# A graph layer on one core: the iota behind the adding gathers of maxima is left out

## The chip, the cores and the metric

The kernel runs on one core of one Trainium2 chip. The metric is the device time of one execution in microseconds (us), from the start of the program to its end. The profile is that of one execution; its span runs from the first to the last instruction.

The core's engines work beside each other, each through its own list of instructions, in order: TensorE (PE; PEld is its weight load), VectorE (DVE), ScalarE (ACT), GpSimd (POOL) and SyncE (SP), which here only issues DMAs. Where one needs another's result it waits on a semaphore.

## The reference

There are 6250 nodes with 256 features and 100000 edges, sorted by destination. For each edge a row of messages is made, and each node takes the maximum over its incoming edges. Then follow a residual sum and a layer norm. Cut to what matters:

```python
x_src = x[src]
x_dst = x[dst]
theta_x = (x_dst - x_src) @ theta_w.T + theta_b
phi_x = x_src @ phi_w.T + phi_b
e = relu(theta_x + phi_x)
out = segment_max(e, dst, num_segments=6250)
out = where(isfinite(out), out, 0.0)
y = x + out
return (y - mean(y)) / sqrt(var(y) + 1e-5)
```

A message is `relu(x_dst @ theta_w.T + x_src @ (phi_w - theta_w).T + theta_b + phi_b)`. The first product is the same for all edges into a node. So the kernel computes B = x @ (phi_w - theta_w).T once for each node, takes the maximum of B's rows over the edges, and adds the other product and the biases to that maximum.

## The kernel before, in words

**Rows of B.** At the start x is loaded, transposed and multiplied, and B is stored to the DRAM tensor `b_rows`. B's rows for single edges are then fetched by gathers: `gather` (L542) issues one indirect DMA on GpSimd's queue, 128 rows of 256 float32 (1 KB each), one row into each partition, chosen by a column of indices.

**Two kinds of nodes.** The first 618 nodes ("part 1" in the code) have their edges cut into 128 chunks of 80 steps; each step is one gather (`gather_group`), and VectorE runs a maximum along the steps (L712). The results go to the DRAM tensor `maxima_1`. The other 5632 nodes are 44 tiles of 128. For these, most edges are handled without a gather: in "slots" of 383 rows of B, at most one edge of each node is picked for each slot, a one-hot matrix is made from the picked rows' codes (ScalarE L1243 and L1247, VectorE L1241), TensorE multiplies it (L1192), and VectorE takes the maximum into `acc` (L1206). What edges are left over form "the list": 128 chunks of 256 steps, again one gather (L543, g<-b_rows,list_src) and one maximum (L712) for each step, stored to `maxima_2`.

**Final part.** For each tile of 128 nodes, `rows_of` (L1465) fetches the node's maximum. Its target is first filled with the bias row (ScalarE, L1478); then a gather with `onto=ALU.add` adds the row of `maxima_1` or `maxima_2` that belongs to each node onto it. These are the *adding gathers*. There are 44 for the tiles of the second kind (g<-maxima,place in the profile), and 5 for the nodes of the first part (x_f<-maxima,place), which `first_shares` (L1707) interleaves with the list. All other gathers use `ALU.bypass`, which copies: the plain gathers.

Then `piece` handles two tiles at a time: TensorE multiplies the transposed x by theta (L1513) and turns `acc` back to rows (L1522), VectorE takes the larger of the gathered row and `acc` (L1523), adds the product (L1524), and adds the relu of it onto x with the row's sum (L1527). `normalise` (L1535) takes squares on ScalarE (L1556), the inverse root on VectorE with a square root on ScalarE (L437 to L444), scales (L1571 on ScalarE, L1567 on VectorE) and stores (L1577; the last share L1551). The shares of the final part are 8, 8, 8, 4, 4, 4, 4, 2 and 2 tiles; loads of x (L1483) and of the transposed x (`kept`, L1463) and the stores go through SyncE's queue.

**What sets the order on GpSimd.** `in_turn` ties each of GpSimd's instructions to the one before, so that they stand as they are written. Behind each gather, from the fifth group of the first part on (`paused[0]`, set in `gather_group`), `gather` puts an iota of 128x160 into a tile `pause` that nobody reads:

```python
pause = const.tile([P, PAUSE], FP, name="pause")
...
if paused[0]:
    in_turn(iota(pause, 1, 0, 0))
```

The profile shows it as IOTA pause (L511, the line of the helper `iota`). Since `paused[0]` stays set, the list's gathers and the adding gathers have it as well.

Of the kernel before, what the change touches and what calls it, by code (L numbers as in the profile page):

```python
# [46 lines left out]
ALU = mybir.AluOpType  # L47
# [400 lines left out]
def gnn_kernel(ctx: ExitStack, tc: tile.TileContext, x, src, dst, theta_w, theta_b, phi_w, phi_b, out):  # L448
# [61 lines left out]
    def iota(t, step, base, per_partition):  # L510
        return nc.gpsimd.iota(  # L511
            t,
            pattern=[[step, t.shape[1]]],
            base=base,
            channel_multiplier=per_partition,
            allow_small_or_imprecise_dtypes=True,
        )
# [9 lines left out]
    def in_turn(one):  # L527
        if latest[0] is not None:
            behind_in_order(one, latest[0], "GpSimd's order")
        latest[0] = one.ins.name  # L530
# [9 lines left out]
    paused = [False]  # L540

    def gather(to, table, offsets, wait_for=None, onto=ALU.bypass):  # L542
        one = nc.gpsimd.indirect_dma_start(  # L543
            out=to, out_offset=None, in_=table, in_offset=bass.IndirectOffsetOnAxis(ap=offsets, axis=0), compute_op=onto
        )
        in_turn(one)
        if wait_for is not None:
            after = mybir.DependencyInfo(mybir.DependencyClass.Sync, mybir.DependencyReason.DATA)
            tc.add_manual_dep(one.ins, wait_for, after, reason="rows that are used")
        issued = latest[0]  # L550
        if paused[0]:
            in_turn(iota(pause, 1, 0, 0))
        return issued

# [15 lines left out]
    def gather_group(i, table, a=0, b=STEPS):  # L570
        paused[0] = i >= PAUSED_FROM
        t0, n = groups[i]
        if i not in ring_tiles:
            ring_tiles[i] = gathered.tile([P, STEPS, D], FP, name="g")
        return [
            gather(ring_tiles[i][:, k, :], table, src_1[:, t0 + k : t0 + k + 1], hold(k)) for k in range(a, min(b, n))
        ]
# [856 lines left out]
    def gather_2(g, t0, a, b):  # L1434
        for k in range(a, b):
            t = LIST_CHUNK - 1 - t0 - k
            gather(g[:, k, :], b_rows, list_src[:, t : t + 1], hold(k))

    def gather_carry():

        carry_row = work.tile([P, D], FP, name="heads", bufs=1)
        gather(carry_row, maxima_2[: 1 + CARRY_GROUPS * STEPS * P, :], carry_at)
        return carry_row
# [408 lines left out]
```

## Time and profile before

| | |
|---|---|
| median of 3 runs | 765.55 us (761.78 to 767.07) |
| the profiled execution | 763.97 us |
| its span | 762.1 us |
| mean granted TensorE clock | 0.948 |
| GpSimd busy | 593.8 us, 78% of the span |
| adding gathers of the final part | 44, from 651.86 us to 741.09 us |

The page gives each engine's busy time, the span in 40 slices, the DMA queues, the chain of work that ended last (followed back from the last instruction, at each step to what released it), and the costliest groups of instructions. A group's row reads: line, engine, operation, what is written <- what is read, x count | busy us, mean ns of one | idle time of the engine ahead of them, and what ended most of it. A row of the timeline reads: start us, duration us, engine, line, operation, tiles, count, and in brackets the idle time ahead of it with its releaser; "issue" is time in which the engine waited for nothing that the profile shows. In rows of waits, "A <- B: 32.5, 15, 4.9" is A waiting for B, in total 32.5 us, 15 times, the longest 4.9 us.

A gather's duration in these rows is the time in which GpSimd issues it. The rows land later; that shows in who waits for them.

### The profile page before, as it was taken

To read this page: it belongs to the slowest core of one execution; us is meant where nothing else is said; L and a number is where in the kernel's file an instruction comes from. 1 tells how busy PE (TensorE), PEld (TensorE's weight loads), DVE (VectorE), ACT (ScalarE), POOL (GpSimd) and SP (SyncE) were. 2 spreads that over 40 slices of the span, in tenths; PEclk is the share of its full clock that TensorE was granted. 3 is DMA by queue.
4 is the path that set the end of the run, shared out by engine and by line. 5 is a ranking of instruction groups with operands and counts; after the bars stand their busy time and mean duration, and the time that the engine had idled before them with its cause. 6 is when DMAs were issued, how large, how long until landed. Compare 5 with 4: busy or idle time off the path is not lost.

```text
span 762.1 us, 9846 instructions
## 1 busy us (share of the span) xinstructions
PE 650.9 (85%) x2837; PEld 525.4 (69%) x2837; DVE 634.4 (83%) x1201; ACT 506.3 (66%) x687; POOL 593.8 (78%) x778
## 2 busy tenths in 40 slices
PE   5898796999989999999898797898887999976730
PEld 3787685878767888888776676676676877865520
DVE  5999899999999999998777787789777987754565
ACT  1444579788985879888766676668475866624545
POOL 7010489998958888888888889888888887799980
PEclk9999999999998999999999998999999999998965
DMA  8896544566469786777777888679678767478763
GB/s 252 286 343 253 177 126 143 150 195 207 152 197 296 238 304 210 244 249 238 244 226 227 269 249 255 198 223 299 210 244 292 243 219 231 92 151 238 168 143 144
DMA packets 66411, 168.22 MB, mean 221 GB/s; under 512 B 11910, under 2 KB 28206, under 8 KB 60206
## 3 DMA queue, kind: packets, MB, share of 16 engines
q1 hardware_dynamic: 40338, 107.92, 41.4%
q0 software_dynamic: 23744, 52.50, 26.5%
q10 hardware_dynamic: 2268, 7.11, 2.5%
q8 instruction: 24, 0.39, 0.2%
q14 instruction: 37, 0.30, 0.1%
HBM read 104.25 MB, written 63.23 MB: 220 GB/s over the span
## 4 chain that ended last, share of the span: by engine, by line
POOL 33%; DVE 22%; PE 18%; issue 12%; DMA 11%; ACT 2%; POOLq 0%; DVEq 0%; ACTq 0%
POOL g L543 25%; PE ps_f L1192 18%; DMA g<-b_rows,list_src 7%; POOL pause L511 7%; DVE g L712 4%; DVE acc L1206 4%; DVE words L1021 2%; DMA g<-maxima,place 2%; DVE hot L1241 2%; DVE work L1018 1%; ACT x_f L1571 1%; DVE work L1376 1%; POOL x_f L543 1%; DVE unused L1083 1%; DMA want<-chosen_rows 1%
## 5 line engine op out<-in xcount | busy, mean ns | idle before, releaser
L1192 PE MATMUL ps_f<-hot,terms 128*128 128x512 f32 x2112 | 507.2, 400 | 44.5 <-DVE acc L1206 32.5
L1192 PEld LDWEIGHTS ps_f<-hot,terms 128*128 128x128 f32 x2112 | 402.7, 193 | 142.6 <-DVE acc L1206 38.2
L543 POOL DMA_INDIRECT g<-b_rows,list_src x256 | 265.1, 1036 | 44.4 <-issue 36.8
L1243 ACT ACTIVATE hot<-want,minus_row 128x1024 fp32r<-128x1024 f16 (+1 forms) x201 | 208.2, 1070 | 110.4 <-PE ps_f L1192 92.6
L1206 DVE SCALAR_TENSOR_TENSOR acc<-ps_f,bias_column,acc 128x1024 f32<-128x1024 f32 (+1 forms) x192 | 227.8, 1190 | 6.4 <-PE ps_f L1192 4.2
L712 DVE SCALAR_TENSOR_TENSOR g<-g,caps 128x256 f32<-128x256 f32 x334 | 159.5, 480 | 59.1 <-DMA g<-b_rows,list_src 43.4
L1247 ACT ACTIVATE hot<-hot 128x1024 fp32r<-128x1024 f32 (+1 forms) x201 | 187.4, 973 | 1.1
L511 POOL IOTA pause<- 128x160 f32 x354 | 140.1, 396 | 2.1
L543 POOL DMA_INDIRECT g<-b_rows,src x72 | 110.2, 1531 | 27.7 <-issue 14.7
L543 POOL DMA_INDIRECT g<-maxima,place x44 | 69.3, 1576 | 13.7 <-issue 7.0
L1241 DVE TENSOR_SCALAR hot<-want,row_id 128x1024 fp32r<-128x1024 f16 (+1 forms) x93 | 67.9, 731 | 6.1 <-PE ps_f L1192 3.8
L811 PE MATMUL ps_b<-weights_b,x_t 128*128 128x256 f32 x228 | 53.8, 390 | 5.4 <-ACT x_t L799 5.2
L811 PEld LDWEIGHTS ps_b<-weights_b,x_t 128*128 128x128 f32 x228 | 43.1, 194 | 12.6 <-ACT x_t L799 7.1
L1513 PE MATMUL ps_f<-weights,kept 128*128 128x256 f32 x128 | 36.2, 432 | 14.3 <-DVE g L1524 8.1
L1513 PEld LDWEIGHTS ps_f<-weights,kept 128*128 128x128 f32 x128 | 26.2, 215 | 19.8 <-issue 15.9
L1556 ACT ACTIVATE squares<-x_f,r 128x256 bf16<-128x256 f32 x47 | 23.2, 494 | 21.2 <-DVE r L1553 21.2
L1523 DVE TENSOR_TENSOR g<-g,ps_f 128x512 f32<-128x512 f32 x16 | 11.0, 686 | 28.6 <-DMA g<-maxima,place 27.7
L1571 ACT ACTIVATE x_f<-x_f,r 128x256 f32<-128x256 f32 x40 | 21.0, 589 | 16.9 <-DVE r L1563 16.8
L814 ACT COPY b_sb<-ps_b 128x512 f32<-128x512 f32 (+1 forms) x25 | 14.4, 578 | 26.4 <-PE ps_b L811 17.8
L1023 POOL MEMSET work<- 128x1584 f32 x1 | 2.3, 2254 | 33.6 <-DVE words L1021 33.6
L799 ACT COPY x_t<-ps_xt 128x512 f32<-128x512 f32 (+1 forms) x29 | 16.1, 584 | 7.8 <-PE ps_xt L795 6.2
L1153 ACT CAST terms<-raw 128x768 fp32r<-128x768 f32 x16 | 13.2, 822 | 11.4 <-PE ps_f L1192 7.3
(275 smaller groups left out, 464.6 us busy)
## 6 DMA issues: line engine op xcount, KB each, us to landing
maxima<-g SPq DMA_DIRECT2D x41, 1024.0 KB
want<-chosen_rows SPq DMA_DIRECT2D x89, 256.0 KB
x_q<-in_x_dram SPq DMA_DIRECT2D x12, 512.0 KB
b_rows<-b_sb ACTq DMA_DIRECT2D x12, 512.0 KB
x_columns<-x_t SPq DMA_DIRECT2D x22, 256.0 KB
kept<-x_columns SPq DMA_DIRECT2D x11, 512.0 KB
raw<-b_rows SPq DMA_DIRECT2D x16, 256.0 KB
g<-b_rows,list_src POOLq DMA_INDIRECT x256
```

The source lines that it names most:

```text
L511: return nc.gpsimd.iota(t, pattern=[[step, t.shape[1]]], base=base, channel_multiplier=per_partition, allow_small_or_imprecise_dtypes=True,)
L543: one = nc.gpsimd.indirect_dma_start(out=to, out_offset=None, in_=table, in_offset=bass.IndirectOffsetOnAxis(ap=offsets, axis=0), compute_ ...
L712: one = nc.vector.scalar_tensor_tensor(g[:, k, :], last[part], caps[:, t : t + 1], g[:, k, :], op0=ALU.min, op1=ALU.max)
L811: nc.tensor.matmul(ps[:, h, :], x_t[:, h, k, :], weights_b[:, k, :], start=(k == 0), stop=(k == KC - 1))
L1192: one = nc.tensor.matmul(ps[:, w : w + 512], terms[:, part, b, h * P : (h + 1) * P], hot[b][:, w : w + 512], start=(i == 0), stop=(i == n ...
L1206: one = nc.vector.scalar_tensor_tensor(to, ps, bias_column[:, h : h + 1], to, op0=ALU.add, op1=ALU.max)
L1241: nc.vector.tensor_scalar(hot[b], want, row_id[:, b : b + 1], None, op0=ALU.is_equal)
L1243: one = nc.scalar.activation(hot[b], want, AF.Abs, bias=minus_row[:, b : b + 1], scale=1.0)
L1247: nc.scalar.activation(apart, apart.bitcast(FP), AF.Relu, bias=1.0, scale=-1.0)
L1513: nc.tensor.matmul(a[:, i, :], x_t[:, 2 * i + c, :], weights[:, c, :], start=(c == 0), stop=(c == KC - 1))
L1556: nc.scalar.activation(squares, x_f[:, k, :], AF.Square, bias=mean[:, k : k + 1], scale=1.0, accum_out=var[:, k : k + 1])
L1571: nc.scalar.activation(x_f[:, k, :], x_f[:, k, :], AF.Identity, bias=mean[:, k : k + 1], scale=inv[:, k : k + 1])
```

## The change

The iota is issued only behind gathers that copy. Behind the adding gathers it is left out; the gathers themselves, their targets and their order stay.

```diff
         issued = latest[0]
-        if paused[0]:
+        if paused[0] and onto == ALU.bypass:
             in_turn(iota(pause, 1, 0, 0))
         return issued
```

This takes 49 of the 354 iotas of `pause` away. GpSimd's order, where the list ends and the final part begins (`maxima_66` is `maxima_2`, `place_704` the places of the nodes' maxima in it); before:

```order
L543 DMA g<-b_rows,list_src 128x256
L511 IOTA pause 128x160
L543 DMA g<-maxima_66,place_704 128x256
L511 IOTA pause 128x160
L543 DMA g<-maxima_66,place_704 128x256
```

and with the change, to the end of the main program (the last two rows read the flag that decides on the general path):

```order
L543 DMA g<-b_rows,list_src 128x256
L511 IOTA pause 128x160
L543 DMA g<-maxima_66,place_704 128x256 x44
L1820 TENSOR_LOAD flags
L1821 COMPARE_AND_BRANCH
```

The 44 adding gathers, an iota between each two before, now follow each other.

In the list stage, on GpSimd too, four of the five adding gathers of the first part's nodes stand together (`maxima_65` is `maxima_1`); with the change:

```order
L543 DMA g<-b_rows,list_src 128x256
L511 IOTA pause 128x160
L543 DMA x_f<-maxima_65,place_703 128x256 x4
L543 DMA g<-b_rows,list_src 128x256
L511 IOTA pause 128x160
```

The iota in front of the four belongs to the list's gather before them; the next one stands behind the list's first gather after them.

## The prediction

> **What bounds the kernel now.** I read the page of the profile first, then GpSimd's own rows over the final part, then who waits for whom there, then the last microseconds. The page gives the span, and the chain of work that ended last.
>
> ```profile
> span 762.1 us, 9846 instructions
> POOL 33%; DVE 22%; PE 18%; issue 12%; DMA 11%; ACT 2%; POOLq 0%; DVEq 0%; ACTq 0%
> POOL g L543 25%; PE ps_f L1192 18%; DMA g<-b_rows,list_src 7%; POOL pause L511 7%; DVE g L712 4%; DVE acc L1206 4%; DVE words L1021 2%; DMA g<-maxima,place 2%; DVE hot L1241 2%; DVE work L1018 1%; ACT x_f L1571 1%; DVE work L1376 1%; POOL x_f L543 1%; DVE unused L1083 1%; DMA want<-chosen_rows 1%
> ```
>
> A third of the chain is GpSimd (POOL), and the iota itself ("pause") has 7% of it. The chain covers all stages, though, and the change touches only the adding gathers, so the stage has to be read by itself. GpSimd's groups from 651.8 to 741.5 us:
>
> ```profile
> L543 POOL DMA_INDIRECT g<-maxima,place x44 | 69.3, 1576 | 13.7 <-issue 7.0 <-ACT hot L1243 6.5 <-ACT x_f L1571 0.2
> L511 POOL IOTA pause<- 128x160 f32 x44 | 38.2, 869 | 0.0
> ```
>
> All 44 adding gathers of the final part lie here, one iota behind each; apart from the 6.5 us ahead of the first one, GpSimd is idle only for the "issue" gaps, 7.0 us over 42 gathers. So nothing holds GpSimd up once it has begun; it runs at its own pace. Who waits for that pace (waits from 651.8 to 745 us):
>
> ```profile
> DVE g L1523 <- DMA g<-maxima,place: 32.5, 15, 4.9
> PE ps_f L1513 <- DVE g L1524: 8.1, 4, 3.1
> ```
>
> VectorE (DVE) works off the rows in 22 pieces of two gathers, and in 15 of the 22 it stands still until the rows have landed, 32.5 us in all. TensorE in turn waits for VectorE to give back its PSUM buffers. Last, the end, in order of time:
>
> ```profile
> 739.53 1.56 POOL L543 DMA_INDIRECT g<-maxima,place  x1 [0.17 <-issue]
> 740.53 0.87 POOL L511 IOTA pause<- 128x160 f32 x1
> 744.46 0.69 DVE L1523 TENSOR_TENSOR g<-g,ps_f 128x512 f32<-128x512 f32 x1 [2.85 <-DMA g<-maxima,place]
> ```
>
> VectorE has been idle for 2.85 us when the last gather's rows are there; 762.1 - 744.5 = 17.6 us of normalising and storing follow. The final part is therefore: 44 gathers at GpSimd's pace, one landing, and a tail of fixed length.
>
> **The change, part by part.** It removes 49 iotas of 128x160, 44 in the final part and 5 behind the gathers into x_f in the list stage, and adds nothing. No wait is added.
>
> First the price of one iota. The recorded 869 ns is not it, as the order of time shows:
>
> ```profile
> 653.92 1.57 POOL L543 DMA_INDIRECT g<-maxima,place  x1 [0.17 <-issue]
> 654.92 0.87 POOL L511 IOTA pause<- 128x160 f32 x1
> 655.95 1.56 POOL L543 DMA_INDIRECT g<-maxima,place  x1 [0.17 <-issue]
> ```
>
> The first gather ends at 653.92 + 1.57 = 655.49; the iota begins on paper at 654.92, inside the gather, and ends at 655.79. Only 0.30 us of it lies behind the gather; then come 0.17 us until the next gather starts. Start to start is 2.03 us, of which 0.30 + 0.17 = 0.47 is not gather.
>
> The Trainium skill, page "Perfetto Trace Analysis", section "GPSIMD Engine Instruction", says to time GpSimd's instructions by the spacing of their starts and not by the recorded duration; the rows above agree (0.87 us recorded, 0.30 outside the gather). By the recorded mean the 43 iotas between gathers would be 37.4 us and the kernel would come to 728.2 us.
>
> What takes the place of the 0.47 us when gather follows gather directly? No adding gather does so in this trace. The nearest rows are plain gathers at the program's start, where no iota stands between:
>
> ```profile
> 5.54 0.95 POOL L543 DMA_INDIRECT g<-in_x_dram,src  x1 [0.30 <-issue]
> 6.79 0.95 POOL L543 DMA_INDIRECT g<-in_x_dram,src  x1 [0.30 <-issue]
> 8.05 0.95 POOL L543 DMA_INDIRECT g<-in_x_dram,src  x1 [0.30 <-issue]
> ...
> 636.88 0.96 POOL L543 DMA_INDIRECT g<-b_rows,list_src  x1 [0.16 <-issue]
> 637.85 0.28 POOL L511 IOTA pause<- 128x160 f32 x1
> 638.29 0.96 POOL L543 DMA_INDIRECT g<-b_rows,list_src  x1 [0.16 <-issue]
> ```
>
> Gather behind gather needs a gap of 0.30 us, start to start 1.25. With the iota it is 1.41. For a plain gather of the same length, the iota costs 1.41 - 1.25 = 0.16 us net, since taking it away brings back a longer issue gap. Applied to the adding gather: 0.47 - 0.30 = 0.165 us. Below, the price of one removed iota is bounded by nothing (the gap grows to 0.47); above by 0.47 (gathers close up altogether). I take 0.165, because the two rows differ from the case in the gather's length alone and the iota's part behind the gather is the same in both, 0.28 and 0.30.
>
> The final part: 43 of the 44 iotas lie between gathers (the one at 740.53 is behind the last and delays nobody): 43 x 0.165 = 7.1 us. The last gather would end at 741.09 - 7.1 = 734.0.
>
> Does what stands behind keep up? A piece would come every 2 x 1.86 = 3.7 us instead of 4.05. VectorE's work for a piece is two operations of 128x512 and two of 128x256, from these groups of the final part:
>
> ```profile
> L1523 DVE TENSOR_TENSOR g<-g,ps_f 128x512 f32<-128x512 f32 x15 | 10.3, 686 | 25.8 <-DMA g<-maxima,place 24.8 <-PE ps_f L1522 0.9
> L1524 DVE TENSOR_TENSOR g<-g,ps_f 128x512 f32<-128x512 f32 x15 | 10.3, 685 | 0.3
> L1527 DVE SCALAR_TENSOR_TENSOR x_f<-g,x_f 128x256 f32<-128x256 f32 x42 | 16.4, 421 | 0.4
> ```
>
> That is 0.69 + 0.69 + 2 x 0.42 = 2.2 us, so 1.5 us of slack are left per piece. Busy times of the two halves of the stage, and of the tail (the columns are PE, PEld, DVE, ACT and POOL busy, TensorE's clock, DMA share, GB/s):
>
> ```profile
> 652.00:700.00 48.00, 40.16 (x192) 33.38 (x190) 27.03 (x75) 21.12 (x48) 44.15 (x48) 0.93 0.70 147
> 700.00:741.00 41.00, 21.88 (x98) 17.25 (x96) 24.21 (x92) 17.42 (x55) 37.66 (x42) 0.83 0.75 178
> 741.00:762.10 21.10, 0.00 (x0) 0.00 (x0) 10.48 (x62) 11.33 (x34) 0.39 (x2) 0.50 0.44 146
> ```
>
> If the second stretch shrinks from 41.0 to 37.7, VectorE is busy 24.2 of it, ScalarE 17.4 and TensorE 21.9; none becomes the bound. TensorE is full early in the first stretch, because leftovers of the slots are multiplied there, but that backlog is gone by the middle. What hides an unfinished piece is VectorE's wait; it shrinks by about a fifth (7.1 of 32.5) and stays. I therefore let the whole 7.1 us reach the end.
>
> The five iotas in the list stage, of which one and four lie behind x_f gathers:
>
> ```profile
> 471.82 1.56 POOL L543 DMA_INDIRECT x_f<-maxima,place  x1 [0.17 <-issue]
> 472.82 0.87 POOL L511 IOTA pause<- 128x160 f32 x1
> 473.85 1.56 POOL L543 DMA_INDIRECT x_f<-maxima,place  x1 [0.17 <-issue]
> ```
>
> The spacing is the same 2.03 us, so 5 x 0.165 = 0.8 us of GpSimd's time. GpSimd is not always the bound there: the chain also runs through landings and VectorE's steps. Between 0 and 0.8 I take 0.4.
>
> Sum: 7.1 + 0.4 = 7.5 us. The span goes from 762.1 to 754.6; with the 1.9 us around it (763.97 - 762.1) the profiled execution would take 756.5. That execution is 1.6 us below the median of the runs shown, 765.55, so against the median I forecast 765.55 - 7.5 = **758.0 us**, a change of 0.98%.
>
> **The rivals.** *Absorbed by the transfers.* A gather's rows land 2.3 to 6.6 us after its end. The two ends of that:
>
> ```profile
> 698.64 1.56 POOL L543 DMA_INDIRECT g<-maxima,place  x1 [0.17 <-issue]
> 706.79 0.69 DVE L1523 TENSOR_TENSOR g<-g,ps_f 128x512 f32<-128x512 f32 x1 [2.93 <-DMA g<-maxima,place]
> ...
> 715.19 1.56 POOL L543 DMA_INDIRECT g<-maxima,place  x1 [0.17 <-issue]
> 719.09 0.69 DVE L1523 TENSOR_TENSOR g<-g,ps_f 128x512 f32<-128x512 f32 x1 [1.88 <-DMA g<-maxima,place]
> ```
>
> Issued until 716.75 and used at 719.09 the second; the first issued until 700.20 and used at 706.79, while tiles of x and of its transposed copy are being loaded. If denser gathers queue up behind such loads to the end, part of the gain goes. For it speaks the DMA share of 0.75; against it, that the lag is back at 744.46 - 741.09 = 3.4 by the last gather. With half the gain lost: 765.55 - 3.75 = 761.8 us.
>
> *The gathers overlap.* The iota starts 0.99 us after its gather's start, inside it. If the next gather may start as early, the 0.30 us gap is hidden too. With half of it hidden, the spacing is 1.71 and the gain 43 x 0.315 = 13.5 us: 752.0 us; fully hidden, 43 x 0.465 = 20 us: 745.6. Against it: behind the iota's early start the spacing repeats at 2.03 without anything running ahead, which looks as if a gather starts only when all before it is complete. The Trainium skill, same page and section, says there is no synchronisation between GpSimd's DSPs except inside instructions, which speaks for this rival.
>
> *Gathers without a gap get slower.* The first part has 25 gathers in a row without iotas (83.9 to 134.6 us), and then 40 with them (134.6 to 214.4 us):
>
> ```profile
> L543 POOL DMA_INDIRECT g<-b_rows,src x25 | 43.4, 1734 | 16.3 <-DMA b_rows<-b_sb 8.9 <-issue 7.3
> L543 POOL DMA_INDIRECT g<-b_rows,src x40 | 59.5, 1488 | 6.6 <-issue 6.6
> ```
>
> The unspaced ones take 0.25 us more. If an adding gather grows as much, its spacing is 1.58 + 0.25 + 0.30 = 2.13, 0.1 above today's: 43 x 0.1 = 4.3 us slower, 769.9 us. It turns the sign as soon as a gather grows by over 0.165 us. Against it: these stretches have different work beside them, and the gathers from x shown above, unspaced as well, take 0.95 us.
>
> That the change does not do what it says is excluded by the order of the instructions: the 44 gathers stand in one run without an iota, and VectorE, TensorE and SyncE keep their sequence.
>
> **How the numbers follow.** Forecast 0.66, with its own range of 6 to 9 us gained, which is 756.5 to 759.6; absorbed 0.15; overlap 0.12; slower 0.07. One per cent is 7.7 us, about what a measurement of this kernel can tell from no change, and the forecast sits right below it. Faster by over 1%: all of the overlap and under half of the forecast, 0.12 + 0.30 = 0.42. Slower by over 1% (a gather growing by 0.35 us) gets 0.04 of the slower rival's 0.07; within 1% is the rest, 0.54. The range 751 to 763 us holds the forecast, the absorbed case's middle and the near end of the overlap; runs of one kernel also lie 5 us apart (761.78 to 767.07).
>
> **What would show it.** Right: adding gathers still 1.56 us, each with 0.30 of issue ahead of it, start to start near 1.86; the last one ends some 89.2 - 7.1 = 82 us after the first starts; VectorE's wait for these rows falls to about 25 us; the tail stays at 17.6. Wrong: a spacing below 1.8 or above 1.95 (overlap, or longer gathers), landings later at the end than 3.4 us, or VectorE waiting for TensorE where it waits for rows now.

## The result and the profile after

The kernel with the change takes 760.27 us (median of 18 runs, 754.29 to 763.24) against 767.11 us before (18 runs, 761.75 to 773.67): ratio 0.9915, 95% interval 0.9891 to 0.994. By the ratio that is 6.5 us, between 4.6 and 8.4. The profiled execution took 760.03 us, with a span of 758.1.

GpSimd's groups over the whole program, after the change:

```profile
L511 POOL IOTA pause<- 128x160 f32 x305 | 97.3, 319 | 2.1
L543 POOL DMA_INDIRECT g<-maxima,place x44 | 69.8, 1586 | 19.9 <-issue 12.8 <-ACT hot L1243 6.8 <-ACT r L439 0.3
```

305 iotas are left, and the gathers' issue gaps have grown from 7.0 to 12.8 us over 42 gathers, 0.30 each. The gathers themselves are as long as before (1586 ns; 1576 then). In order of time on GpSimd and VectorE, with the first gather, three that follow, the last one, and the use of its rows:

```profile
653.50 1.59 POOL L543 DMA_INDIRECT g<-maxima,place  x1 [6.77 <-ACT hot L1243]
655.39 1.56 POOL L543 DMA_INDIRECT g<-maxima,place  x1 [0.30 <-issue]
657.26 1.55 POOL L543 DMA_INDIRECT g<-maxima,place  x1 [0.30 <-issue]
659.11 1.55 POOL L543 DMA_INDIRECT g<-maxima,place  x1 [0.30 <-issue]
...
734.85 1.56 POOL L543 DMA_INDIRECT g<-maxima,place  x1 [0.31 <-issue]
740.42 0.69 DVE L1523 TENSOR_TENSOR g<-g,ps_f 128x512 f32<-128x512 f32 x1 [3.29 <-DMA g<-maxima,place]
```

Start to start is 1.86 us in the median of the 43 spacings (1.85 to 2.11); it was 2.03. The first gather starts at 653.50 and the last ends at 736.41: 82.9 us, where it was 89.2. What VectorE waits for in that time (waits from 640 to 745 us):

```profile
DVE g L1523 <- DMA g<-maxima,place: 24.9, 14, 6.1
```

It still waits for rows, now 24.9 us instead of 32.5. The two traces laid beside each other:

| | before | after | |
|---|---|---|---|
| first adding gather of the final part starts | 651.86 | 653.50 | +1.6 |
| from there to the last one's end | 89.2 | 82.9 | -6.3 |
| from there until VectorE uses its rows | 3.4 | 4.0 | +0.6 |
| from there to the end of the span | 17.6 | 17.7 | 0.0 |
| span | 762.1 | 758.1 | -4.0 |

These two executions differ by less than the medians do, because the final part began 1.6 us later in the second one. Single executions differ by several us: the 18 of the kernel before lie between 761.75 and 773.67, and the final part starts at 646.8 to 653.5 us in the six profiles here, one for each kernel, that keep the iotas behind plain gathers. So time to the final part is judged by many runs, and the final part by its own length.

### The profile page after: what moved, and what is told of

Same layout as the page of the kernel before. It is cut to its first block, busy times and chain, and to the rows that moved or that the text cites. A ratio compares the mean times of both kernels' runs of the same rounds, so it can differ in the third digit from the quotient of the medians.

```text
span 758.1 us, 9797 instructions
## 1 busy us (share of the span) xinstructions
PE 652.5 (86%) x2837; PEld 525.5 (69%) x2837; DVE 635.4 (84%) x1201; ACT 506.7 (67%) x687; POOL 583.7 (77%) x729
## 5 line engine op out<-in xcount | busy, mean ns | idle before, releaser
L543 POOL DMA_INDIRECT g<-b_rows,src x72 | 112.6, 1564 | 27.5 <-issue 14.7
L511 POOL IOTA pause<- 128x160 f32 x305 | 97.3, 319 | 2.1
L543 POOL DMA_INDIRECT g<-maxima,place x44 | 69.8, 1586 | 19.9 <-issue 12.8
L811 PE MATMUL ps_b<-weights_b,x_t 128*128 128x256 f32 x228 | 55.5, 399 | 4.2 <-ACT x_t L799 4.0
L1523 DVE TENSOR_TENSOR g<-g,ps_f 128x512 f32<-128x512 f32 x16 | 11.0, 687 | 22.5 <-DMA g<-maxima,place 22.5
```

Source lines behind the costliest of these rows:

```text
L511: return nc.gpsimd.iota(t, pattern=[[step, t.shape[1]]], base=base, channel_multiplier=per_partition, allow_small_or_imprecise_dtypes=True,)
L543: one = nc.gpsimd.indirect_dma_start(out=to, out_offset=None, in_=table, in_offset=bass.IndirectOffsetOnAxis(ap=offsets, axis=0), compute_ ...
L811: nc.tensor.matmul(ps[:, h, :], x_t[:, h, k, :], weights_b[:, k, :], start=(k == 0), stop=(k == KC - 1))
```

## Experiments

**Only the final part.** The 44 iotas of the final part go, the five in the list stage stay:

```diff
-        if paused[0]:
+        if paused[0] and not (onto == ALU.add and table is maxima_2):
```

> Only the 44 iotas of the final part are left out; the five in the list stage stay. Theory (the adding gathers' spacing falls from 2.03 to 1.86 us, and all of that reaches the end): first adding gather's start to the last one's end 82.9 us instead of 89.2, tail unchanged, 6.3 us faster, ratio near 0.992, the same as the full change. Rival (part of the gain is the list stage's): about 5.5 us or less, ratio 0.993 or above, and the final part's time still 6.3 us shorter.

Measured: 758.61 us against 766.39, ratio 0.9883 (0.9853 to 0.9912). First and last adding gather of the final part:

```profile
653.26 1.59 POOL L543 DMA_INDIRECT g<-maxima,place  x1 [6.50 <-ACT hot L1243]
733.41 1.55 POOL L543 DMA_INDIRECT g<-maxima,place  x1 [0.30 <-issue]
```

81.7 us from first start to last end. The final part alone gives all that the whole change gives, within the measurement; the two ratios' intervals overlap. By its ratio this kernel gains 9.0 us (6.7 to 11.3), more than the 6.3 that were expected; its final part is 7.5 us shorter in the profile, and its last rows are used 1.3 us later. What the rest of the 9.0 us would be is not shown; this kernel ran six times.

**Only the list stage.** The opposite: the five go, the 44 stay.

```diff
-        if paused[0]:
+        if paused[0] and not (onto == ALU.add and table is maxima_1):
```

> Only the five iotas behind the gathers into x_f are left out; the 44 of the final part stay. Theory: nothing that can be measured, -0.8 to 0 us, ratio 0.999 to 1.000, since GpSimd is not always what the list waits for. Rival (the order of landings in the list is changed for the worse, which would explain that the final part began 1.6 us later in the profiled execution of the change): ratio 1.002 and the final part's first gather later than 652 us again.

Measured: 765.08 us, ratio 0.9982 (0.9959 to 1.0006), the final part 89.4 us as before. The first adding gather of the final part:

```profile
646.82 1.59 POOL L543 DMA_INDIRECT g<-maxima,place  x1 [6.22 <-ACT hot L1243]
```

It starts early in this execution, at 646.8, not late, and the kernel above, which keeps the five, starts late, at 653.26. So nothing shows that leaving the five out delays the list; the 1.6 us of the table above lie within what single executions differ by. A gain of up to 0.8 us is neither shown nor excluded.

**Two iotas instead of one** behind the adding gathers:

```diff
-        if paused[0]:
+        for _ in range(2 if paused[0] and onto == ALU.add else paused[0]):
```

> Two iotas instead of one behind each of the 49 adding gathers. Theory (each iota adds its own issue time behind the gather, and the gather's pace sets the final part): the second iota lengthens the spacing by 0.16 to 0.30 us, so the final part is 7 to 13 us longer and the kernel 0.9 to 1.7 per cent slower, microsecond for microsecond with the spacing. Rival (the pace is partly hidden behind landings): the spacing grows as much, but the kernel loses less than half of it.

Measured: 782.23 us, ratio 1.0228 (1.0182 to 1.0275), which is 14 to 21 us slower. The final part on GpSimd:

```profile
659.38 1.56 POOL L543 DMA_INDIRECT g<-maxima,place  x1 [0.15 <-issue]
660.37 1.19 POOL L511 IOTA pause<- 128x160 f32 x2
661.71 1.55 POOL L543 DMA_INDIRECT g<-maxima,place  x1 [0.15 <-issue]
```

Start to start is 2.33 us, 0.30 more than with one iota. The second iota thus costs all of its 0.30 us, while the first costs only 0.17 net, since it stands in the place of the 0.30 us gap. From first start to last end it takes 104.6 us, 15.4 more than before, and the median grew by 15.8: microsecond for microsecond. That is more than the 7 to 13 us of final part that were expected: the spacing grew by the most that had been allowed for, 0.30 us, and some spacings are longer still, up to 3.47 us.

**An iota of one column** in place of 160, behind the adding gathers:

```diff
-            in_turn(iota(pause, 1, 0, 0))
+            in_turn(iota(pause[:, :1] if onto == ALU.add else pause, 1, 0, 0))
```

> Behind the 49 adding gathers the iota writes one column (128x1) instead of 160; behind the plain ones it stays. What is the 0.30 us of an iota made of? Theory (most of it is the iota's own run over its columns): start to start of the adding gathers is 1.75 to 1.90 us, near or even below that without an iota, and the kernel gains 5 to 12 us on the one before, ratio 0.985 to 0.993. Rival (it is the cost of one more instruction, whatever its size): spacing 2.00 us as before, ratio 0.998 to 1.002.

Measured: 761.63 us against 766.9, ratio 0.9938 (0.9907 to 0.9969). That is 4.8 us by the ratio, just short of the 5 to 12 that were expected; the final part is 5.7 us shorter, 83.5 instead of 89.2. On GpSimd:

```profile
660.25 1.56 POOL L543 DMA_INDIRECT g<-maxima,place  x1 [0.16 <-issue]
661.25 0.72 POOL L511 IOTA pause<- 128x1 f32 x1
662.13 1.55 POOL L543 DMA_INDIRECT g<-maxima,place  x1 [0.16 <-issue]
```

Start to start is 1.88 us, 0.02 above no iota at all (by the medians 1.89 and 1.86). So of the 0.17 us that the iota costs here, 0.15 are its run over the other 159 columns; an instruction of one column in the place of the gap is nearly free. The record gives this iota 0.72 us. The Trainium skill's "Perfetto Trace Analysis", section "GPSIMD Engine Instruction", advises to go by the spacing of starts; here the record is over twenty times the cost.

**No iota at all:**

```diff
-        if paused[0]:
+        if False:
```

> No iota behind any gather. Theory (a plain gather is 1.25 us apart without the iota and 1.41 with it, and nothing else changes): GpSimd saves 0.16 x 354 = 57 us, of which TensorE, busy nine tenths of the list stage, lets 10 to 35 us through: ratio 0.955 to 0.987. Rival (plain gathers without a gap get slower, as the 25 unspaced ones of the first part, or crowd out the other engines' transfers): list gathers of 1.3 us and more instead of 1.04, or the steps that read them longer, and the kernel not faster, ratio 0.995 to 1.03.

Measured: 716.56 us, ratio 0.9343 (0.9309 to 0.9377), 50 us faster, more than expected. GpSimd's group of the list's gathers:

```profile
L543 POOL DMA_INDIRECT g<-b_rows,list_src x256 | 268.4, 1049 | 80.4 <-issue 49.7 <-DVE acc L1206 11.1 <-DVE g L712 8.6
```

The plain gathers take 1049 ns without an iota between them and took 1036 with it: they hardly get slower. VectorE's wait for their rows, from 240 to 600 us:

```profile
DVE g L712 <- DMA g<-b_rows,list_src: 5.7, 6, 1.6
```

It was 37.5 us before. The list's first gather and the first adding gather of the final part, in order of time:

```profile
241.16 1.28 POOL L543 DMA_INDIRECT g<-b_rows,list_src  x1 [0.30 <-DVE g L712]
...
611.53 1.59 POOL L543 DMA_INDIRECT g<-maxima,place  x1 [7.82 <-ACT g L1478]
```

That is 370 us, where it was 651.9 - 239.1 = 413. TensorE's work in that stage is the new floor, as the windows show: the whole list stage of the kernel before, and 160 us of the stage without iotas (columns as in the prediction):

```profile
239.00:645.00 406.00, 371.83 (x1570) 297.61 (x1568) 338.40 (x566) 288.04 (x339) 358.65 (x525) 0.97 0.76 245
...
320.00:480.00 160.00, 157.66 (x690) 129.00 (x689) 148.88 (x245) 127.62 (x148) 124.24 (x118) 0.99 0.86 275
```

The stage before had 372 us of TensorE work in it. I had taken that as a limit that lets 10 to 35 us through; it lets 42 through, and next to nothing of TensorE's idle time is left: it is busy 157.66 of the 160 us.

The 48 iotas behind the first part's gathers were worth nothing. Those 72 gathers take 154.2 us from the first start to the last end before and 153.6 without iotas; VectorE is busy 155.94 of the 156 us from 84 to 240 us in both.

**The iota behind the adding gathers alone**, none behind plain ones:

```diff
-        if paused[0]:
+        if paused[0] and onto == ALU.add:
```

> The opposite of the change: the iota stays behind the 49 adding gathers and is left out behind all plain ones. Theory (each stage gives its own part, and the parts add): final part as before, 89 us from the first adding gather's start to the last one's end; kernel 6.3 us slower than without any iota, 723 us, ratio 0.942 to 0.944. Rival (with the list sped up, something else sets the final part, so that its iotas are hidden): 717 us, ratio 0.935.

Measured: 722.76 us, ratio 0.9426 (0.9373 to 0.948). Its first and last adding gather of the final part:

```profile
609.82 1.59 POOL L543 DMA_INDIRECT g<-maxima,place  x1 [8.43 <-ACT g L1478]
...
697.88 1.56 POOL L543 DMA_INDIRECT g<-maxima,place  x1 [0.17 <-issue]
```

The final part takes 89.6 us again. Against the run without any iota that is 6.2 us, the size of the change in a kernel whose list ends 42 us earlier. The two parts add, in the ratios too: 0.0085 less by the change and 0.0574 less here make 0.0659, where no iota at all has 0.0657.

**Plain gathers in the final part.** If GpSimd's pace sets the final part, a shorter gather must bring more than the iota did. The bias, which the adding gather had in its target, is added by TensorE:

```diff
-            nc.scalar.copy(rows[:, :filled, :], bias_row.to_broadcast([P, filled, D]))
...
-            gather(m[:, k, :], maxima, places[:, j0 + k : j0 + k + 1], onto=ALU.add)
+            gather(m[:, k, :], maxima, places[:, j0 + k : j0 + k + 1])
...
+                nc.tensor.matmul(a[:, i, :], ones_row, bias_row[0:1, 0, :], start=False, stop=True)
...
-                    to, ps, bias_column[:, h : h + 1], to, op0=ALU.add, op1=ALU.max
+                    to, ps, 0.0, to, op0=ALU.add, op1=ALU.max
```

> No iota at all, and the 49 adding gathers are plain ones too: no target is filled with the bias row, the slots' maxima are taken without it, and TensorE adds it in the final part's product, by one more matmul of one row for each tile. Theory (GpSimd's pace of 1.86 us an adding gather sets the final part, and a plain gather's is 1.25): GpSimd is done 44 x 0.6 = 27 us earlier, but a piece of two tiles then comes every 2.5 us, and TensorE (2.2 us and two more matmuls) and VectorE (2.2 us and the norms) take over, so that 15 to 22 us of it reach the end: 695 to 702 us, ratio 0.907 to 0.916. Rival (landings set the pace, as their waits say): less than 8 us, 709 us or more, ratio 0.925 or above.

Measured: 707.51 us, ratio 0.9224 (0.9161 to 0.9287), 9 us better than without any iota, and a miss: less than forecast. GpSimd was done with its gathers in 55.2 us, at 658.74, but TensorE was full. One stretch of it in the windows:

```profile
655.00:690.00 35.00, 35.00 (x150) 21.57 (x148) 24.77 (x99) 20.40 (x64) 2.84 (x3) 1.00 0.48 171
```

TensorE is busy all 35 us of it; GpSimd has three gathers left. Accordingly VectorE now waits for TensorE and not for rows (waits from 610 to 700 us; L1522 and L1521 are L1523 and L1522 of the other kernels):

```profile
DVE g L1522 <- PE ps_f L1521: 18.3, 16, 2.4
```

And two rows of order of time on TensorE and its weight loads:

```profile
640.59 0.29 PEld L1514 LDWEIGHTS ps_f<-bias_row,ones_row 1*128 1x128 f32 x2 [0.33 <-issue]
640.60 0.69 PE L1514 MATMUL ps_f<-bias_row,ones_row 1*128 1x256 f32 x2
```

The gain is not the final part's. Its first gather, in order of time:

```profile
603.55 0.95 POOL L543 DMA_INDIRECT g<-maxima,place  x1 [8.61 <-DMA maxima<-g]
```

Without any iota it was at 611.53. So 8.0 us of the 9 are gained ahead of the final part, and from this gather to the end of the span it takes 102.9 us, only 1.1 less than there (104.0). Why it starts earlier was not tried; the list already starts 4.6 us earlier, and that start lies between 236.3 and 241.2 us in the profiles of all these kernels.

A piece came every 3.76 us, set by TensorE. I had put the two bias matmuls at little; they cost about 1.6 us of it (3.76 less the 2.2 of a piece without them), 0.69 us of record each, with 0.33 us of idle time ahead of the weight loads. Two runs tested that. In the first the bias matmul is left out, and with it the bias:

> As the kernel with plain gathers only, but the matmul that adds the bias is left out, so the output lacks the bias. Theory (with plain gathers TensorE had become the bound, 3.76 us a piece, and the bias matmul's two weight loads and four passes were 1.6 us of it): TensorE is back at 2.2 us a piece, VectorE with its norms (2.5 us) and GpSimd (2.5 us) set the pace together, the final part shrinks by 25 to 30 us against the kernel with plain gathers: 678 to 684 us, ratio 0.884 to 0.892. Rival (landings of the gathers set the pace once TensorE does not): VectorE waits for them as before, 690 us or more, ratio 0.90 or above.

Measured: 680.83 us, ratio 0.8887 (0.881 to 0.8964), as the theory has it. Pieces come every 2.2 to 2.3 us at the end, and from the first gather (601.37 us) to the end of the span it is 77.4 us, 26.5 less than without any iota, where GpSimd's gathers are done 26.3 us sooner. In the second the bias is added by a cheaper matmul:

```diff
-    ones_row = const.tile([1, P], FP, name="ones_row")
+    ones_row = const.tile([96, P], BF, name="ones_row")
+    bias_parts = const.tile([96, D], BF, name="bias_parts")
...
+        left = bias_row[:, 0]
+        for i in range(3):
+            rounded = prep.tile([P, D], BF, name=f"rounded{i}")
+            nc.scalar.copy(rounded, left)
+            nc.scalar.copy(bias_parts[32 * i : 32 * i + 1, :], rounded[32 * i : 32 * i + 1, :])
+            if i < 2:
+                rest = prep.tile([P, D], FP, name=f"rest{i}")
+                nc.vector.tensor_tensor(rest, left, rounded, op=ALU.subtract)
+                left = rest
...
-                nc.tensor.matmul(a[:, i, :], ones_row, bias_row[0:1, 0, :], start=False, stop=True)
+                nc.tensor.matmul(a[:, i, :], ones_row, bias_parts, start=False, stop=True)
```

Not shown are the fills of the two tiles with ones and zeros, and a smaller `PAUSE`, the size of a tile that nothing uses here.

> As the kernel with plain gathers only, but the bias is added by a bf16 matmul with the bias split into three bf16 parts on three rows (their sum is the float32 bias), zeros on the rows between. Theory (the cost of the bias matmul was its float32 passes and weight loads): 0.3 to 0.45 us a tile instead of 0.8, a piece every 2.8 to 3.1 us, 685 to 694 us, ratio 0.893 to 0.905, the fastest complete kernel of these. Rival (switching types and weights costs TensorE the same 0.8 us a tile): 705 to 708 us, ratio 0.92.

Measured: 679.91 us against 766.42, ratio 0.8854 (0.8795 to 0.8914), the fastest complete kernel of these and faster than forecast (685 to 694 us). TensorE's group for the bias, from 620 to 660 us:

```profile
L1525 PE MATMUL ps_f<-bias_parts,ones_row 96*128 96x256 bf16 x24 | 6.6, 274 | 0.0
```

The first gather of the final part and VectorE's last piece, in order of time (L1533 is L1523 of the kernel before):

```profile
604.32 0.95 POOL L543 DMA_INDIRECT g<-maxima,place  x1 [7.70 <-DMA maxima<-g]
...
666.35 0.69 DVE L1533 TENSOR_TENSOR g<-g,ps_f 128x512 f32<-128x512 f32 x1
```

The bias matmul takes 0.27 us of record, and from the first gather to the last piece it is 62 us instead of 92.6 in the kernel before. The record is again not the price. In order of time on TensorE:

```profile
638.53 0.28 PE L1525 MATMUL ps_f<-bias_parts,ones_row 96*128 96x256 bf16 x1
638.64 0.60 PE L1532 MATMUL ps_f<-ident,acc 128*128 128x128 f32 x4
```

The next matmul starts 0.11 us after it. By starts a piece takes TensorE 2.40 us here and 2.17 without the bias, so the bias costs 0.11 to 0.12 us a tile. The forecast's 0.3 to 0.45 was too high; over 44 tiles that is 8 to 15 us, which accounts for the faster kernel. Type and number of rows were changed at once; which of them makes it cheap was not tried.

## Why the prediction was right, point by point

*The bound.* Right. The final part went at GpSimd's pace, and the runs that changed that pace changed the kernel by about as much: fewer iotas (6.2 and 6.5 us), more (15.8 us, the final part 15.4), a shorter one (4.8 us, the final part 5.7). A shorter gather changed the final part hardly at all while TensorE was full (1.1 us), and by 26.5 and 28.4 us when the bias matmul was left out or cheap.

*The price of an iota.* Right: 0.165 us was forecast, and the spacing went from 2.03 to 1.86. It did come from the plain gathers' gap of 0.30 us, which an adding gather needs as well. That the gap would carry over from one kind of gather to the other was an assumption, and it held.

*43 iotas, 7.1 us.* Right. The three profiles with the iota (before, only the list, only behind adding gathers) have 89.2, 89.4 and 89.6 us from the first start to the last end; the three without (the change, only the final part, none at all) 82.9, 81.7 and 82.6. The means differ by 7.0 us.

*All of it reaches the end.* Not quite; one of the prediction's signs of being wrong, a landing later at the end than 3.4 us, did come. The last rows were used 3.4, 3.4 and 3.5 us after the last gather with the iota, and 4.0, 4.7 and 3.9 without it: 0.8 us on the mean are lost to later landings. I had weighed this as a rival that eats half; it eats a ninth. With two iotas the lag was 2.4 us and with the one-column iota 4.6, so among the adding gathers it grows as the spacing shrinks. In the trace of the change a store of the finished rows is issued from 734.4 us on, next to the last gather at 734.85; that it holds up the landing is only a guess from that, not tried.

*The list stage, 0.4 us.* Open: 0.9982 with an interval from 0.9959 to 1.0006 for the five alone. The term was the middle between nothing and 0.8, and no run shows it.

*The sum.* 7.5 us were forecast, 6.5 (4.6 to 8.4) measured. 7.0 - 0.8 = 6.2 us is what the final part shows. The forecast of 758.0 us is 2.3 below the median measured. Some 1.6 of that come from the median before, 767.11 in the 18 runs where the forecast started from 765.55; the other 0.7 is the gain, 6.8 us by the medians alone.

*The rivals.* Gathers without a gap do not get slower: 1586 ns against 1576 for the adding ones, 1049 against 1036 for the list's. The 25 long unspaced gathers spoke for it, but a missing gap alone does not make gathers that long: the 40 behind them, 1.49 us each on the mean with iotas, take 1.55 us without iotas in one profile (no iota at all) and 1.31 in another (only behind adding gathers). What did make the 25 long was not tried. Overlap is excluded as well: the spacing is never below 1.84 us with 1.54 us gathers, so each starts about 0.30 us after the one before has ended. The Trainium skill, page "Perfetto Trace Analysis", section "GPSIMD Engine Instruction", says that GpSimd's DSPs are not synchronised except inside instructions; if a gather could start in an earlier one's last part, these rows would show it, and they do not.

*Where I looked too narrowly.* I saw that the iota had 7% of the chain, and that a plain gather is 1.25 us apart without it and 1.41 with it. For the 305 iotas that the change leaves this says 305 x 0.16 = 49 us of GpSimd's time. The runs show about 44 at the end: a ratio of 0.9343 without any iota, 0.9915 with the change. But the sum over all of them comes near that partly by luck: the list's 256 alone make 41 us, and the list stage lost 42, while the first part's 48 brought nothing.

## What to carry to other kernels

Price a small instruction on GpSimd by the spacing of starts around it, with and without it, and not by its recorded duration; subtract the gap that comes back when it goes. Where one engine issues in a row and the others wait for what it issues, its spacing times the count is the stage, until the next engine's work per step is reached; work that one out too, its weight loads included. And when the same row prices a part that a change leaves alone, do that sum as well, stage by stage.

## What the runs showed of the hardware

An indirect gather of 128 rows of 1 KB kept GpSimd for 0.95 us in most rows of the list and of the final part when it copies (1.53 us on the mean of the first part's 72), and for 1.56 us when it adds, with 0.30 us between two of either kind. A float32 matmul of a single row by 256 columns cost TensorE about 0.8 us among others of 128 rows, 0.69 us by the record; a bf16 one of 96 rows cost 0.11 to 0.12, with a record of 0.27.
